# Order of work around the last norms, the memory block's projection and its outputs in a two-layer decoder kernel

## The chip, the cores and the metric

The kernel runs on one core of a Trainium2 chip. The core has TensorE (PE in the profile; PEld is its loading of weights), VectorE (DVE), ScalarE (ACT), GpSimd (POOL) and SyncE (SP, which here issues nearly all transfers). The metric is device time in microseconds, the median over runs.

## The reference, cut to what matters

All is f32, 2048 tokens (32 sequences of 64) of width 512. Four blocks follow each other, each added to x, each fed by a layer norm of x:

```python
x = x + L0_xattn(layernorm(x), ctx)      # 32 query heads, 8 key heads, RoPE, softmax over 64 keys
x = x + L0_ffn(layernorm(x))             # int4 weights, 512 -> 1376 -> 512, silu(gate) * up
x = x + L1_xattn(layernorm(x), ctx)      # q and k with RMS norms per head
x = x + L1_ffn(layernorm(x))             # the memory block:

def L1_ffn(h):
    query = h @ Wq.T                                      # 64 wide
    router = (query @ Wr.T) @ (keys @ Wr.T).T / sqrt(48) + log_rel    # over 128 slots
    top = top_k(router, 8)
    w = softmax(query @ keys.T / 8 + log_rel, over top)
    aux = (w @ values) @ Wvd.T @ Wvu.T
    log_var = log1p(var(h))
    learned = gelu(h @ Wu1.T + bu1) @ Wu2.T + bu2
    u = clip(0.5 * log_var / mean(log_var) + 2.5 * sigmoid(learned), 0, 5)
    gate = sigmoid(w1 * clip((u - 0.5) / 1.5, 0, 1) + bias)   # 0 where under 0.05
    return h + gate * aux
```

The mean of log_var runs over all 2048 tokens, so no gate is known before the last norm.

## The kernel before, in words

The tokens are cut into four chunks of 512 (index c, 0 to 3), each of four tiles of 128 tokens. x stays on the chip. An attention walks 32 steps (g, c): for each of 8 groups g of heads, the four chunks. Large products (the query projection and the output projection) are made as seven half-size products instead of eight (`product`, L179, with PE's matmuls on line L186; `quarters`, L195), which needs sums of blocks of the operands: `left_sums` (L163) and `right_sums` (L171), four additions on POOL each.

One step of `run` (L635) works on several steps at once. In PE's order it has: the rest of the output products of the step before (40 matmuls O), the key projection pk (`project_k`) and the query projection P (56 matmuls, `project_q`) of the next step, the weighted values po of this step (`values`, L554), the small sums pm for the RMS norms of the next step (`norms`, L433), its value projection pv, the first two output products O of this step (16 matmuls, `output_first`), and the scores S of the next step (`scores`, L462). `norms` has DVE add epsilon (qs, L458), POOL raise to the power -1/2 (qr, `rsqrt`, L229) and DVE spread the queries' part to a tile rb (L278). `softmax` (L479) is a generator whose pieces are run between the output products of `output_rest` (L601): it scales S by rb and a key's column (L504), POOL adds the mask (L514), DVE takes the maximum, ACT the exponential (L540), POOL multiplies by the reciprocal sums (L546).

In the last group's steps the chunks are finished one after the other. When chunk c has its last output product, `joined(c)` makes the memory block's values of chunk c-1 (`mem_values`, pwt and paux on PE) and the norm's statistics of chunk c; `after(c)` then runs `norm_apply` (L246) and `mem_weights` (L1009) for chunk c. For chunk 3 both stand behind the attention, and then come the gates and the outputs (`mem_gate`, `mem_out`). `norm_apply` has DVE make a normed tile xn (L251), PE transpose it (L256) and ACT copy it to xnT (L260), and then calls `mem_each` for that tile: DVE's variance of xn (L1002, L1003) and POOL's addition of xn to x (L1004). `mem_weights` projects xnT to qy (pqy, on L1014, copied on L1025) and to the gate's hidden layer (pu, same line), makes the slot scores pr (L1031), the gelu (L1035) and its product with one column (pl, L1038; copied to lrn, L1041), and then the choice of the top eight slots on DVE (L1046 to L1058). `mem_softmax` has DVE take the maximum (L1069) and ACT the exponential (L1072). `mem_mean`, in chunk 3, takes the mean of log_var (L1101 on ACT, L1103 on PE). `mem_out` writes out = aux * gate + x by one DVE instruction a tile (L1148) and sends it (L1151); the 12 tiles of chunks 0 to 2 share gate "a", the four of chunk 3 gate "b", whose aux is still in PSUM.

The program is written with a tile framework. It takes the instructions in program order as priorities, plays them through by a cost model, and so fixes for each engine an order in which that engine issues; an engine then takes its instructions strictly in that order. It also adds the semaphores and gives out buffers. `tc.issue_after(ins)` adds to each instruction of its block that runs on the engine of `ins` the condition that it be ordered behind `ins`; it adds no wait. Tiles of the kind m2 (512 wide) share four buffers.

Of the kernel before, what the change touches and what calls it, by code (L numbers as in the profile page):

```python
# [15 lines left out]
ALU = mybir.AluOpType  # L16
# [28 lines left out]
def tile_xattn_ffn_2_layers(ctx: ExitStack, tc: tile.TileContext, a: dict, out: bass.AP):  # L45
# [125 lines left out]
    def right_sums(t):  # L171
# [4 lines left out]
        tt(b[1], b[3], b[1], ALU.subtract)  # L176
        tt(b[6], b[2], b[5], ALU.subtract)

    def product(which, ps, left, right, widths=(P, P), first=True):  # L179


        l, r = PRODUCTS[which]
        pv = ps.rearrange("p (m n) -> p m n", m=2)
        for m, w in enumerate(widths):
            for k in range(2):
                nc.tensor.matmul(  # L186
                    pv[0:w, m, :],
                    left[:, l, k, m * P : m * P + w],
                    right[:, r, k, :],
                    start=(first and m == 0 and k == 0),  # L190
                    stop=(k == 1),
                    skip_group_check=True,
                )

    def quarters(n, left, right, done, widths=(P, P)):  # L195

# [29 lines left out]

    def rsqrt(dst, src):

        nc.gpsimd.tensor_tensor(dst, src, nhalf[:, : src.shape[-1]], ALU.pow)  # L229

    norms = {}

# [13 lines left out]
    def norm_apply(c, name, each=None):  # L246

        mv, rs = norms[c]
        for t in range(TT):
            xn = m2_tile(f"xn{name}{c}_{t}")  # L250
            ins = nc.vector.tensor_scalar(  # L251
                xn, x_sb[c][:, t, :], mv[:, t, 0:1], rs[:, t : t + 1], ALU.subtract, ALU.mult
            )
            pt = mm_tile(f"xt{name}{c}_{t}")
            for k in range(KT):
                nc.tensor.transpose(  # L256
                    pt[:, k * P : (k + 1) * P], xn[:, k * P : (k + 1) * P], ident
                )
            at = (t % 2) * P
            nc.scalar.copy(  # L260
                xnT[c][:, t // 2 : 4 : 2, :, at : at + P],
                pt.rearrange("p (j k t) -> p j k t", j=2, k=2),
            )
            if each is not None:
                each(c, t, xn)
        if each is None:
            right_sums(xnT[c])
        return ins.ins

# [17 lines left out]
    class Attention:  # L287
        def __init__(self, layer):
            self.L = layer
            self.wq, self.wkv, self.wo = {}, {}, {}  # L290
            self.names = (
                ("L0_wq", "L0_wk", "L0_wv", "L0_wo")
                if layer == 0
                else ("L1_wqT", "L1_wkT", "L1_wvT", "L1_woT")
            )
# [137 lines left out]
        def norms(self, g, c, kpart, part):  # L433


            if self.L == 0:
                return None
            n = f"1_{g}_{c}"
            NQ, NK = NH * GQ * KH, NH * KH

            pm = mm_tile(f"pm{n}")
            k6 = kpart.rearrange("p (x j) -> p j x", j=4)
            p6 = part.rearrange("p i f (j x) -> p j i f x", j=4)
            for j in range(4):
                nc.tensor.matmul(
                    pm[j * KB : (j + 1) * KB, 0:NQ].rearrange("p (f i x) -> p i f x", f=NH, i=2),
                    fold,
                    p6[:, j],
                    start=True,
                    stop=True,  # L450
                )
                nc.tensor.matmul(
                    pm[j * KB : (j + 1) * KB, NQ : NQ + NK], fold, k6[:, j], start=True, stop=True
                )
            qs = sm.tile([P, NQ + NK], F32, tag="qs", name=f"qs{n}")
            qr = sm.tile([P, NQ + NK], F32, tag="qr", name=f"qr{n}")

            nc.vector.tensor_scalar(qs, pm[:, 0 : NQ + NK], HD * EPS, None, ALU.add)  # L458
            rsqrt(qr, qs)
            return spread(f"rb{n}", qr[:, 0:NQ]), qr[:, NQ:]  # L460

        def scores(self, g, c, kT, qT):  # L462
            n = f"{self.L}_{g}_{c}"
# [15 lines left out]
        def softmax(self, g, c, st, scales):  # L479
# [18 lines left out]
                src = s5  # L498
                scale = 1.0 / math.sqrt(HD)
            else:  # L500
                rb, kr = scales
                for f in range(NH):
                    for e in range(KH):
                        nc.vector.scalar_tensor_tensor(  # L504
# [130 lines left out]
        def run(self, hooks, joined, after, between=lambda c: None, tail=lambda: None, late={}):  # L635
# [15 lines left out]
            for i, (g, c) in enumerate(steps):  # L651
# [38 lines left out]
                oT = self.values(g, c, v, probs)  # L690
                if more:
                    scales = self.norms(*steps[i + 1], kpart, part)
                self.pooled = left_sums(oT)
                if more:
                    v = self.project_v(*steps[i + 1], ctxT)
                before = self.output_first(g, c, oT)
                if more:
                    st = self.scores(*steps[i + 1], kT, qT)
                ctxT = ctx_next
            between(NCH - 2)  # L700
            self.output_rest(*before)
# [306 lines left out]

    def mem_weights(c, behind=lambda: None):  # L1009

        def project(ps, w):
            for half in range(2):
                for k in range(KT):
                    nc.tensor.matmul(  # L1014
                        ps[:, half * HC : (half + 1) * HC],
                        w[:, k, :],
                        xnT[c][:, 2 * (k // 2) + half, k % 2, :],
                        start=(k == 0),
                        stop=(k == KT - 1),
                    )  # L1020
# [3 lines left out]
        qy = m2_tile(f"qy{c}")  # L1024
        nc.vector.tensor_copy(qy[0:BOT, :], py[0:BOT, :])  # L1025
        p = mm_tile(f"pu1_{c}")
        project(p, mem["wu1"])
        behind()
        pr = st_tile(f"pr{c}").rearrange("p j (t n) -> p (j t) n", t=2)
        for t in range(TT):  # L1030
            nc.tensor.matmul(  # L1031
                pr[:, t, :], qy[0:BOT, t * P : (t + 1) * P], mem["m2"], start=True, stop=True
            )
        gT = m2_tile(f"gT{c}")
        nc.scalar.activation(gT, p, AF.Gelu_apprx_tanh, bias=mem["bu1"])  # L1035
        pl = mm_tile(f"pl{c}")
        for t in range(TT):
            nc.tensor.matmul(  # L1038
                pl[:, t : t + 1], gT[:, t * P : (t + 1) * P], mem["wu2"], start=True, stop=True
            )  # L1040
        nc.vector.tensor_copy(mem["lrn"][:, c * TT : (c + 1) * TT], pl[:, 0:TT])  # L1041
        bc = [P, TT, NSLOT]
        lr = mem["lr"].unsqueeze(1).to_broadcast(bc)

# [14 lines left out]
            att, left, neg[:, 1:2].unsqueeze(2).to_broadcast(bc)  # L1059
        )  # L1060
        mem["att", c] = att

    def mem_softmax(c, behind=None):
        if behind is not None:
# [68 lines left out]
    def mem_out(name, c0, c1):  # L1133
# [4 lines left out]
        for c in range(c0, c1):  # L1138
            o4 = (
                q_tile(f"o{c}")  # L1140
                if c == 0
                else (o_tile if c == 1 else w_tile)(f"o{c}")[:, 0:4].rearrange("p b h w -> p b (h w)")
            )
            for t in range(TT):
                g = c * TT + t
                col = g - c0 * TT
                o = o4[:, t, :]
                nc.vector.scalar_tensor_tensor(  # L1148
                    o, mem["aux", c, t], gate[:, col : col + 1], x_sb[c][:, t, :], ALU.mult, ALU.add
                )  # L1150
                nc.sync.dma_start(out[g * P : (g + 1) * P, :], o)  # L1151


# [43 lines left out]
    def load_second():  # L1197
# [12 lines left out]
    )  # L1210
    att1.run(
        {(0, 1): [lambda: norm_apply(last, "c")], (1, 0): [lambda: mem_constants(att1.loaded)]},
        lambda c: (mem_values(c - 1) if c > 0 else None, norm_stats(c, "d")),
        lambda c: (norm_apply(c, "d", mem_each), mem_weights(c)),
        lambda c: mem_softmax(c, att1.copied),
    )
    norm_apply(last, "d", mem_each)
    mem_weights(last, mem_mean)
    mem_gate("a", 0, last)
    mem_softmax(last)  # L1220
    mem_values(last)
# [82 lines left out]
```

## Time and profile before

| what | value |
|---|---|
| median of 3 runs | 2943.01 us (2938.76 to 2943.08) |
| the profiled execution | 2943.32 us, of which the span is 2941.5 |
| PE busy | 2838.8 us, 97% |
| mean granted PE clock | 0.987 |
| one ordinary step of the second attention | 36.15 us (pk to pk) |
| last output instruction ends | 2938.31 us |

An instruction's line starts with its start and its duration in us; "xcount" says how many are merged, and the bracket gives the engine's idle time before it and what ended it. Tiles carry their chunk's work in their names: xnd are the normed tiles of the memory block's norm, xtd their transposes. The tail, from about 2750 us on, has chunk 0's norm at 2756, chunk 1's at 2817, chunk 2's at 2865 and chunk 3's at 2905.

### The profile page before, as it was taken

To read this page: it belongs to the slowest core of one execution; us is meant where nothing else is said; L and a number is where in the kernel's file an instruction comes from. 1 tells how busy PE (TensorE), PEld (TensorE's weight loads), DVE (VectorE), ACT (ScalarE), POOL (GpSimd) and SP (SyncE) were. 2 spreads that over 40 slices of the span, in tenths; PEclk is the share of its full clock that TensorE was granted. 3 is DMA by queue.
4 is the path that set the end of the run, shared out by engine and by line. 5 is a ranking of instruction groups with operands and counts; after the bars stand their busy time and mean duration, and the time that the engine had idled before them with its cause. 6 is when DMAs were issued, how large, how long until landed. Compare 5 with 4: busy or idle time off the path is not lost.

```text
span 2941.5 us, 40415 instructions
## 1 busy us (share of the span) xinstructions
PE 2838.8 (97%) x16502; PEld 2217.1 (75%) x16502; DVE 1812.1 (62%) x2752; ACT 820.2 (28%) x1397; POOL 1283.9 (44%) x932
## 2 busy tenths in 40 slices
PE   7999999999999999899999999999999999999987
PEld 5878787778887787676666677777777777787765
DVE  7667777777777766544433665555555555555565
ACT  3323333333333333211111222222222222222232
POOL 5544545454545455411222444444445353535432
PEclk9999999999999999899999999999999999999998
DMA  4111111111111111000000102120202020201001
GB/s 159 40 44 44 52 45 51 49 60 51 45 52 44 51 44 58 23 22 22 20 8 17 36 29 67 34 65 30 65 29 65 30 65 29 65 31 64 15 1 58
DMA packets 103807, 130.71 MB, mean 44 GB/s; under 512 B 8725, under 2 KB 65165, under 8 KB 103623
## 3 DMA queue, kind: packets, MB, share of 16 engines
q1 hardware_dynamic: 103047, 127.09, 13.3%
q8 instruction: 130, 2.13, 0.3%
q10 hardware_dynamic: 576, 1.05, 0.1%
q14 instruction: 54, 0.44, 0.1%
HBM read 123.92 MB, written 4.19 MB: 44 GB/s over the span
## 4 chain that ended last, share of the span: by engine, by line
PE 80%; DVE 12%; ACT 3%; issue 2%; POOL 2%; DMA 0%; DVEq 0%; ACTq 0%; POOLq 0%
PE P L186 30%; PE O L186 22%; PE pv L369 8%; PE pk L339 6%; PE pd L896 5%; PE S L470 4%; DVE part L425 2%; PE po L566 2%; DVE x L592 2%; DVE qT L419 1%; ACT q L421 1%; ACT rq L384 1%; DVE S L493 1%; PE pqy L1014 1%; DVE r2x L525 1%
## 5 line engine op out<-in xcount | busy, mean ns | idle before, releaser
L186 PE MATMUL P<-xnT,wq 128*128 128x256 f32 x3584 | 799.2, 382 | 23.4 <-ACT h L209 21.9
L186 PE MATMUL O<-wo,oT 128*128 128x256 f32 x3584 | 803.8, 382 | 4.2 <-ACT oT L574 3.3
L186 PEld LDWEIGHTS P<-xnT,wq 128*128 128x128 f32 x3584 | 678.8, 191 | 159.2 <-issue 39.2
L186 PEld LDWEIGHTS O<-wo,oT 128*128 128x128 f32 x3584 | 671.4, 190 | 118.0 <-issue 22.1
L592 DVE TENSOR_TENSOR x<-x,O 128x512 f32<-128x512 f32 (+1 forms) x448 | 368.5, 823 | 145.6 <-PE O L186 145.1
L546 POOL TENSOR_TENSOR s<-s,ib 128x512 f32<-128x512 f32 x128 | 169.6, 1347 | 489.0 <-DVE ib L278 480.5
L209 ACT COPY h<-P 128x512 f32<-128x512 f32 (+1 forms) x352 | 200.1, 573 | 365.4 <-PE P L186 354.5
L388 POOL TENSOR_TENSOR qT<-h,rq 128x512 f32<-128x512 f32 x128 | 175.4, 1370 | 277.1 <-DVE rq L387 267.2
L186 PE MATMUL P<-xnT,wgu 128*128 128x256 f32 (+1 forms) x1232 | 273.8, 382 | 0.0
L540 ACT ACTIVATE s<-s 128x1024 f32<-128x1024 f32 x64 | 67.7, 1057 | 708.1 <-DVE s L538 708.1
L186 PEld LDWEIGHTS P<-xnT,wgu 128*128 128x128 f32 (+1 forms) x1232 | 228.0, 187 | 47.1 <-issue 7.4
L229 POOL TENSOR_TENSOR qr<-qs,nhalf 128x20 f32<-128x20 f32 x32 | 113.4, 3543 | 335.0 <-DVE qs L458 335.0
L369 PE MATMUL pv<-wkv,ctxT 128*128 128x128 f32 x1984 | 238.0, 278 | 3.0 <-DVE h L401 1.7
L369 PEld LDWEIGHTS pv<-wkv,ctxT 128*128 128x128 f32 x1984 | 226.2, 192 | 14.0 <-issue 8.6
L384 ACT COPY rq<-h 64x512 f32<-64x512 f32 x256 | 157.9, 617 | 245.3 <-DVE h L401 242.9
L339 PE MATMUL pk<-ctxT,wkv 128*128 128x512 f32 x496 | 223.1, 592 | 0.0
L419 DVE TENSOR_TENSOR qT<-h,P 128x512 f32<-128x512 f32 x128 | 83.9, 674 | 170.4 <-PE P L186 170.4
L885 POOL TENSOR_TENSOR hT<-h,h 128x512 f32<-128x512 f32 (+1 forms) x48 | 55.6, 1179 | 283.4 <-DVE h L878 263.7
L339 PEld LDWEIGHTS pk<-ctxT,wkv 128*128 128x128 f32 x496 | 94.1, 190 | 92.9 <-issue 89.9
L896 PE MATMUL pd<-wd,hT 128*128 128x512 f32 (+1 forms) x352 | 155.0, 592 | 0.0
L386 DVE TENSOR_TENSOR h<-h,cosT 128x512 f32<-128x512 f32 x128 | 90.0, 703 | 105.0 <-ACT rq L384 105.0
L878 DVE TENSOR_TENSOR h<-h,P 128x512 f32<-128x512 f32 (+1 forms) x96 | 59.6, 640 | 151.9 <-PE P L186 103.7
(235 smaller groups left out, 3234.4 us busy)
## 6 DMA issues: line engine op xcount, KB each, us to landing
ctxT<-in_ctxT SPq DMA_DIRECT2D x62, 1024.0 KB
wq<-in_L_wq SPq DMA_DIRECT2D x32, 256.0 KB
wo<-in_L_wo SPq DMA_DIRECT2D x32, 256.0 KB
wq<-in_L_wqT SPq DMA_DIRECT2D x32, 256.0 KB
wo<-in_L_woT SPq DMA_DIRECT2D x32, 256.0 KB
wgu<-in_qweight_gu SPq DMA_DIRECT2D x40, 128.0 KB
out<-o SPq DMA_DIRECT2D x16, 256.0 KB
x<-in_x SPq DMA_DIRECT2D x12, 256.0 KB
```

The costliest lines, as they stand in the source:

```text
L186: nc.tensor.matmul(pv[0:w, m, :], left[:, l, k, m * P : m * P + w], right[:, r, k, :], start=(first and m == 0 and k == 0), stop=(k == 1), ...
L209: nc.scalar.copy(t[size], ps[size])
L229: nc.gpsimd.tensor_tensor(dst, src, nhalf[:, : src.shape[-1]], ALU.pow)
L339: nc.tensor.matmul(ps, wkv[:, k, 0, :], ctxT[:, k, :], start=(k == 0), stop=(k == KT - 1))
L369: nc.tensor.matmul(ps[:, t * HD : (t + 1) * HD], ctxT[:, k, t * P : (t + 1) * P], wkv[:, k, 1, :], start=(k == 0), stop=(k == KT - 1),)
L384: nc.scalar.copy(t[lo:hi, 1], src[HD - hi : HD - lo])
L388: nc.gpsimd.tensor_tensor(dst(None), dst(x), dst(t[:, 1]), ALU.add)
L419: nc.vector.tensor_tensor(q, xv, yv, ALU.add)
L470: nc.tensor.matmul(s5[j * KB : (j + 1) * KB, f, e], kT[:, f, e, j], qT[:, f * 4 + j].rearrange("p h q -> p (h q)"), start=True, stop=True,)
L546: nc.gpsimd.tensor_tensor(sv[:, f], sv[:, f], ib[:, f * W : (f + 1) * W].unsqueeze(1).to_broadcast([P, KH, W]), ALU.mult,)
L592: self.added = nc.vector.tensor_tensor(dst, dst, src, ALU.add).ins
L896: nc.tensor.matmul(p, hT[0:w_, t, tk * P : (tk + 1) * P], wd[i][0:w_, t, :], start=(t == 0), stop=(t == len(tiles) - 1),)
```

## The change

- `norm_apply` with `each` (the memory block's norms alone): all four tiles are normed, transposed and copied first, and `mem_each` is called for the four behind them.
- `mem_weights`: the slot scores pr (and in chunk 3 the mean's part) come between the two halves of the gate's projection pu. The gelu's result lies in block 0 of the chunk's xnT instead of an m2 buffer. Its product pl becomes a function of its own, `mem_learned`, called ahead of the chunk's `mem_values`, that is in `joined(c + 1)`, and for chunk 3 behind `mem_weights`.
- `norms` returns the column tile; the spread rb is made in `softmax`, ordered behind the latest addition of an output product on DVE.
- In `run`, the scores are ordered behind the latest product's last matmul, and in the second attention the sums of oT behind the next step's power on POOL.
- `mem_out`: of gate "a", the first tile of each chunk is made on POOL by two instructions instead of one on DVE.

```diff
     def norm_apply(c, name, each=None):
@@
-            if each is not None:
+            tiles.append(xn)
+        if each is not None:
+            for t, xn in enumerate(tiles):
                 each(c, t, xn)
-        if each is None:
+        else:
             right_sums(xnT[c])
@@ norms
-            rsqrt(qr, qs)
-            return spread(f"rb{n}", qr[:, 0:NQ]), qr[:, NQ:]
+            self.pooled = rsqrt(qr, qs)
+            return qr[:, 0:NQ], qr[:, NQ:]
@@ softmax
-                rb, kr = scales
+                qr, kr = scales
+                if self.added is None:
+                    rb = spread(f"rb{n}", qr)
+                else:
+                    with tc.issue_after(self.added):
+                        rb = spread(f"rb{n}", qr)
@@ run
-                self.pooled = left_sums(oT)
+                if self.L == 1 and more:
+                    with tc.issue_after(self.pooled):
+                        self.pooled = left_sums(oT)
+                else:
+                    self.pooled = left_sums(oT)
@@
-                    st = self.scores(*steps[i + 1], kT, qT)
+                    with tc.issue_after(last_matmul):
+                        st = self.scores(*steps[i + 1], kT, qT)
@@ mem_weights
-        project(p, mem["wu1"])
-        behind()
         pr = st_tile(f"pr{c}").rearrange("p j (t n) -> p (j t) n", t=2)
-        for t in range(TT):
-            nc.tensor.matmul(
-                pr[:, t, :], qy[0:BOT, t * P : (t + 1) * P], mem["m2"], start=True, stop=True
-            )
-        gT = m2_tile(f"gT{c}")
+
+        def scores():
+            behind()
+            for t in range(TT):
+                nc.tensor.matmul(
+                    pr[:, t, :], qy[0:BOT, t * P : (t + 1) * P], mem["m2"], start=True, stop=True
+                )
+
+        project(p, mem["wu1"], scores)
+
+        gT = blocks(c, 0)
         nc.scalar.activation(gT, p, AF.Gelu_apprx_tanh, bias=mem["bu1"])
-        pl = mm_tile(f"pl{c}")
-        for t in range(TT):
-            nc.tensor.matmul(
-                pl[:, t : t + 1], gT[:, t * P : (t + 1) * P], mem["wu2"], start=True, stop=True
-            )
-        nc.vector.tensor_copy(mem["lrn"][:, c * TT : (c + 1) * TT], pl[:, 0:TT])
+        mem["gT", c] = gT
@@
+    def mem_learned(c):
+
+        pl = mm_tile(f"pl{c}")
+        for t in range(TT):
+            nc.tensor.matmul(
+                pl[:, t : t + 1], mem["gT", c][:, t * P : (t + 1) * P], mem["wu2"], start=True, stop=True
+            )
+        nc.vector.tensor_copy(mem["lrn"][:, c * TT : (c + 1) * TT], pl[:, 0:TT])
@@ mem_out
-                nc.vector.scalar_tensor_tensor(
-                    o, mem["aux", c, t], gate[:, col : col + 1], x_sb[c][:, t, :], ALU.mult, ALU.add
-                )
+                if name == "a" and t == 0:
+
+                    aux = mem["aux", c, t]
+                    nc.gpsimd.tensor_scalar(aux, aux, gate[:, col : col + 1], None, ALU.mult)
+                    nc.gpsimd.tensor_tensor(o, aux, x_sb[c][:, t, :], ALU.add)
+                else:
+                    nc.vector.scalar_tensor_tensor(
+                        o, mem["aux", c, t], gate[:, col : col + 1], x_sb[c][:, t, :],
+                        ALU.mult, ALU.add,
+                    )
                 nc.sync.dma_start(out[g * P : (g + 1) * P, :], o)
@@ the calls
-        lambda c: (mem_values(c - 1) if c > 0 else None, norm_stats(c, "d")),
+        lambda c: ((mem_learned(c - 1), mem_values(c - 1)) if c > 0 else None, norm_stats(c, "d")),
@@
     mem_weights(last, mem_mean)
+    mem_learned(last)
     mem_gate("a", 0, last)
```

## The prediction

> **What bounds the kernel now.** I read the page first, then the waits of PE by stretch, then timelines of one ordinary step and of the tail.
>
> ```profile
> PE 2838.8 (97%) x16502; PEld 2217.1 (75%) x16502; DVE 1812.1 (62%) x2752; ACT 820.2 (28%) x1397; POOL 1283.9 (44%) x932
> ...
> PEclk9999999999999999899999999999999999999998
> ```
>
> PE is busy 97% at nearly full clock, so only a PE gap or work after PE's last matmul can be won. The waits of PE, first for second-attention steps without memory work (1700 to 2740 us), columns: total, times, longest:
>
> ```profile
> PE pm L445 <- DVE part L425: 10.9, 29, 0.6
> ```
>
> and for the tail (2740 to 2942):
>
> ```profile
> PE xtd L256 <- DVE xnd L251: 10.9, 5, 4.6
> PE xtd L256 <- DVE vst L1003: 6.0, 4, 2.0
> PE pwt L1083 <- ACT xnT L1072: 5.7, 1, 5.7
> PE paux L1088 <- ACT wT L1085: 4.0, 4, 1.3
> PE O L186 <- ACT oT L574: 2.1, 1, 2.1
> PE pl L1038 <- ACT gT L1035: 0.7, 3, 0.3
> ```
>
> 29 ordinary steps share 10.9 us of waits that the change doesn't touch; the last 200 us hold 29.4. An ordinary step in the timeline:
>
> ```profile
> 2254.57 0.71 DVE L278 STREAM_TRANSPOSE rb<-qr 128x512 f32<-128x512 f32 x1 [3.66 <-POOL qr L229]
> ...
> 2256.18 0.69 DVE L592 TENSOR_TENSOR x<-x,O 128x512 f32<-128x512 f32 x1 [0.90 <-PE O L186]
> ...
> 2257.80 1.93 PE L470 MATMUL S<-qT,kT 128*32 128x256 f32 x32
> ...
> 2257.91 0.69 DVE L592 TENSOR_TENSOR x<-x,O 128x512 f32<-128x512 f32 x1 [1.04 <-PE O L186]
> ...
> 2259.80 1.66 DVE L504 SCALAR_TENSOR_TENSOR s<-S,qr,rb 128x256 f32<-128x256 f32 x4 [1.21 <-PE S L470]
> ```
>
> S already stands behind the second product, POOL's power (2251.00) ahead of the sums of oT (2254.51).
>
> **The pins and the moved spread: 0.** The spread rb goes behind the second addition (ends 2258.60), so it ends at 2259.31; S ends at 2259.73, L504 starts at 2259.80. Its cover is 0.4 us. Without it L504 comes up to 0.7 us later, still off PE: the weights are ready at 2275.0, and po needs them at about 2284 (15.7 us behind pk, as one step earlier). The sums wait for the power as they do now, layer 0's scores stand behind the second product already, and no DMA moves.
>
> **Norm tiles first.** Chunk 2 in the timeline:
>
> ```profile
> 2864.97 1.00 DVE L251 TENSOR_SCALAR xnd<-x,mvd,rsd 128x512 f32<-128x512 f32 x2 [1.14 <-POOL rsd L229]
> ...
> 2865.59 2.73 POOL L1004 TENSOR_TENSOR x<-x,xnd 128x512 f32<-128x512 f32 x2 [0.66 <-DVE xnd L251]
> ...
> 2867.16 1.45 DVE L251 TENSOR_SCALAR xnd<-x,mvd,rsd 128x512 f32<-128x512 f32 x1
> ```
>
> The third tile takes 1.45 us instead of 0.5: it is through only when POOL's additions are, at 2868.32. DVE and POOL exclude each other here. Around 1707 us three such tiles ran against four POOL operations, taking turns: 3.67 us for three, POOL 1.45 each instead of 1.27. The variances (L1002, 0.65 each) no longer stand between, but POOL's additions still start with the first tile. So the fourth tile is gained only in part. Chunks 0 and 1: its end goes from 2761.24 to about 2760.1, -1.15 each. Chunk 2: third tile -1.2, fourth -0.3, PE transposing at half clock between: -0.7. Chunk 3: -0.45. Sum **-3.45** (ends 0, if the turns fall otherwise, and -6, if POOL never got in the way). The variances end about 1 us later (chunk 3: 2912 instead of 2910.9); behind them Ln has its result near 2914, and PE asks for it after half the gate's projection, near 2915.3.
>
> **Slot scores amid the projection, gelu's product later.** Each half of the projection takes 1.86 us. pr (1.99) needs qy, copied 0.8 us after the first projection: ready. The top-eight chain on DVE starts 1.86 earlier and gelu 1.99 later, which nothing waits for any more. PE no longer waits for gT: **-0.7** (last row of the waits). pl (1.05, 8 matmuls) moves, it doesn't vanish: for chunk 0 it goes between two busy stretches (0); for chunk 1 into the 4.6 us in which PE waits for chunk 2's norm (-1.05); for chunk 2 either into the gap before O or ahead of pwt, where it is paid again (-1.05 or 0; I take -0.5). Sum **-1.55**. In chunk 2 an exponential of the gate (L1116, waiting for lrn until 2885.64) stands ahead of ACT's oT copies: they start at 2885.76, though po ended at 2884.79 and an ordinary step has 0.07 between. With lrn made later that goes: **-0.9** (0 if pl stays early). The earlier top-eight chain brings power, mask and exponential about 1 us earlier against PE, so wT is no longer behind it on ACT: two paux waits fall from 1.28 to the 0.73 seen at 2902.17, and chunk 2's statistics gain some 0.5: **-1.6** (ends 0, -2.2).
>
> **The end.** In chunk 3 pr ends at 2919.56, its DVE chain sets the exponential, PE's 5.7 us wait and the outputs. It will come ahead of half a projection (1.86); I take 0.25 off, because PE then changes operands twice: **-1.6** beside the norm's share (ends 0, if DVE is held otherwise, and -1.86).
>
> From 2926.42 DVE writes the outputs without a break:
>
> ```profile
> 2935.59 2.73 DVE L1148 SCALAR_TENSOR_TENSOR o<-paux,g_gateb,x 128x512 f32<-128x512 f32 x4 [0.24 <-DVE g_gateb L1137]
> ```
>
> 16 of them take 11.9 us to 2938.31, then 3.2 us for the last transfer. Three go to POOL: -2.1. But each becomes two POOL operations: an addition of 1.27 (L1004) and a scaling that has no row. Its nearest rows are the two-input 128x512 at 1.27 above and a one-input 128x128 selection at 0.30 below (four of them 1.2); I take 1.2, ends 0.3 and 1.27. Six make 7.4 us. A DVE form like the output's, two tensors and a scalar column, shows what they do to it, once free and once against POOL's L546:
>
> ```profile
> 348.04 0.70 DVE L745 SCALAR_TENSOR_TENSOR scales_gu<-scales_gu,pidx 12x512 f32<-12x512 bf16 x1
> ...
> 350.18 1.64 DVE L745 SCALAR_TENSOR_TENSOR scales_gu<-scales_gu,pidx 12x512 f32<-12x512 bf16 x1
> ```
>
> So the POOL operations hold up outputs and gate b's small scalings between them. Of 7.4 about 1.0 overlaps (a held one ends 0.54 behind POOL, not 0.70): +6.4. With the three outputs saved: **+4.3** (ends -2.1 and +5.3). SP issues the 16 transfers in order, 0.33 each; POOL is through about 10 us after the gate, 6 before the last output, so its three hold up none at the end. The Trainium skill (GPSIMD Engine Reference, Elementwise — side-by-side cycle accounting) gives 769 ns for its best loop on 512 elements; by that estimate the three scalings are 1.3 us cheaper and the sum 1.3 lower. No run here shows it.
>
> **The clock.** Columns: PE, PEld, DVE, ACT, POOL busy, granted clock, DMA, GB/s.
>
> ```profile
> 2754.40:2767.30 12.90, 8.53 (x34) 5.42 (x33) 7.65 (x16) 3.60 (x6) 5.33 (x4) 0.74 0.00 1
> ...
> 2884.80:2891.30 6.50, 4.44 (x12) 3.52 (x13) 3.98 (x14) 3.79 (x13) 3.36 (x3) 0.74 0.00 0
> ```
>
> After gaps of 2.17 and 0.92 the clock lost 0.26 x 12.9 = 3.4 us, after one of 2.07 1.7 us. Chunk 0, chunk 1 and the O gap lose 8.5 together. Shorter gaps should save part: **-1.5** (ends -6 and +1.7, one stretch more). The Trainium skill (TensorE: Matmul & The Clock Gate, What's actually happening) has the slow clock come after an idle window of about 3.4 us. By that rule gaps of 2 us would cost nothing and this term would be 0, the sum 2937.8; the second row, slow after a gap of 2.07 us, speaks against it, and 2937.8 lies in the forecast's own range.
>
> **Sum.** -3.45 - 1.55 - 0.7 - 0.9 - 1.6 - 1.6 - 1.5 + 4.3 = -7.0. The profiled execution took 2943.3 (span 2941.5 and 1.8 around it), 0.3 above the median of 2943.0: 2943.3 - 7.0 = **2936.3**.
>
> **Rivals.** *POOL costs nothing at the end*: its operations fall beside outputs without holding them, end term -2.1: 2943.3 - 11.3 - 2.1 = 2929.9. For it: 12 output rows ran with no POOL beside them, so this line never met it; against: L745. *Gains given back*: only norm tiles, gelu wait and pl count (-5.7), because the order on DVE and ACT in the tail puts other waiting work in front, and the end takes its full +5.3: 2942.9. For it: ACT's L1116 shows such queueing now. *Slower*: the pin says only that S comes behind the second product. If S drifts behind all of O, it moves 8.7 us (2259.7 to 2268.4), and the 9.0 us that the softmax weights now have before po shrink to 0.3. On its way stand 7 us of DVE work for q and k; if that adds 1.2, PE waits 0.9 in each of 31 steps: 2936.3 + 28 = 2964. It decides for slower from 0.42 us a step, (2949.2 - 2936.3) / 31. Against: S now stands there unpinned in every ordinary step.
>
> **Chances.** About 0.2% (5.9 us) is what a measurement of this kernel tells from no change: the three times spread over 4.3. Forecast 0.50 (own range 2931 to 2941), end free 0.14, given back 0.27, S late 0.09. Faster than 2937.1: 0.36 of the forecast, 0.13 of the second, 0.03 of the third: 0.52. Slower than 2948.9: 0.09 and 0.02 of given back: 0.11. Within: 0.37. Range 2930 to 2945: it takes in the first three.
>
> **What would show it.** S still behind 16 O matmuls and rb behind the second L592; four xnd in about 3.8 us with POOL's additions stretched; pr between two runs of eight pu; no PE wait for gT; oT copies right behind po in chunk 2; 13 DVE outputs, several of 1.3 to 2 us, beside six POOL operations. I am wrong if the outputs keep 0.74 us, if PE's wait for xnd or the clock's slow stretches grow, or if ordinary steps are no longer 36.15 us.

## The result, and the profile after

The changed kernel takes **2932.76 us** (median of 7 runs, 2929.51 to 2934.91); the kernel before 2941.91 (7 runs, 2938.76 to 2943.36). The ratio is 0.9969, with a 95% interval of 0.9958 to 0.9981: 9.1 us less, between 5.6 and 12.4. The prediction was 2936.3, 7.0 less. The profiled execution took 2932.82, with a span of 2931.0; before it was 2943.32 and 2941.5.

The page of the changed kernel, engines and clock:

```profile
PE 2837.0 (97%) x16502; PEld 2215.4 (76%) x16502; DVE 1811.8 (62%) x2749; ACT 819.9 (28%) x1397; POOL 1292.6 (44%) x938
...
PEclk9999999999999999899999999999999999999998
```

PE does the same matmuls in 1.8 us less. POOL has six instructions more and 8.7 us more. The waits of PE, first in the ordinary steps (1700 to 2735 us), columns: total, times, longest:

```profile
PE pm L453 <- DVE part L433: 10.7, 29, 0.4
```

That was 10.9 before: nothing has happened there. Then in the tail (2735 to 2931):

```profile
PE xtd L261 <- DVE xnd L256: 11.3, 10, 2.9
PE paux L1116 <- ACT wT L1113: 2.8, 4, 0.7
PE pl L1086 <- ACT xnT L1059: 2.1, 1, 2.1
PE pwt L1111 <- ACT xnT L1100: 1.6, 1, 1.6
PE O L189 <- ACT oT L587: 1.1, 1, 1.1
PE xtd L261 <- ACT xnT L265: 0.8, 1, 0.8
```

These are 19.7 us where 29.4 stood. The wait for the variances (vst, 6.0) is gone; the transposes wait for scaled tiles and, once, 0.8 us for a copy to xnT. The wait for the exponential in chunk 3 (pwt) went from 5.7 to 1.6, with a new one of 2.1 ahead of it: pl, now behind the gelu, waits for it. In chunks 0 to 2 that wait is gone.

Chunk 2's norm in the timeline of the changed kernel (start, time, engine, line, work; in brackets what was waited for):

```profile
2856.65 3.83 DVE L256 TENSOR_SCALAR xnd<-x,mvd,rsd 128x512 f32<-128x512 f32 x4 [1.13 <-POOL rsd L233]
2857.27 5.56 POOL L1022 TENSOR_TENSOR x<-x,xnd 128x512 f32<-128x512 f32 x4 [0.66 <-DVE xnd L256]
...
2857.34 1.08 PE L261 MATMUL xtd<-ident,xnd 128*128 128x128 f32 x8 [2.89 <-DVE xnd L256]
...
2859.21 1.09 PE L261 MATMUL xtd<-ident,xnd 128*128 128x128 f32 x4 [0.79 <-ACT xnT L265]
...
2860.39 1.27 DVE L1020 BATCH_NORM_STATS2 st<-xnd 128x6 f32<-128x512 f32 x2
```

The four tiles follow each other, but need 3.83 us, as POOL's additions begin 0.6 us behind the first. From the first scaled tile to the first matmul of pqy the four chunks took 6.46, 6.47, 5.66 and 4.86 us before, and take 5.16, 5.16, 4.99 and 4.54 now.

At the end, the outputs on DVE, with the small operations of gate b between them:

```profile
2912.54 0.75 DVE L1182 SCALAR_TENSOR_TENSOR o<-xnT,g_gatea,x 128x512 f32<-128x512 f32 x1
...
2915.61 0.74 DVE L1182 SCALAR_TENSOR_TENSOR o<-xnT,g_gatea,x 128x512 f32<-128x512 f32 x1
...
2917.00 1.23 DVE L1145 TENSOR_SCALAR g_sgb<-g_sgb 128x4 f32<-128x4 f32 x1
2918.14 1.83 DVE L1182 SCALAR_TENSOR_TENSOR o<-xnT,g_gatea,x 128x512 f32<-128x512 f32 x1
...
2923.99 2.73 DVE L1182 SCALAR_TENSOR_TENSOR o<-paux,g_gateb,x 128x512 f32<-128x512 f32 x4 [0.24 <-DVE g_gateb L1165]
```

and POOL beside them:

```profile
2912.60 3.95 POOL L1179 TENSOR_SCALAR xnT<-xnT,g_gatea 128x512 f32<-128x512 f32 x2 [13.13 <-DVE g_ub L1152]
2916.52 2.90 POOL L1180 TENSOR_TENSOR o<-xnT,x 128x512 f32<-128x512 f32 x2
2919.41 2.00 POOL L1179 TENSOR_SCALAR xnT<-xnT,g_gatea 128x512 f32<-128x512 f32 x1
2921.49 1.44 POOL L1180 TENSOR_TENSOR o<-xnT,x 128x512 f32<-128x512 f32 x1
```

The first output starts at 2912.5, where it started at 2926.4: **13.9 us earlier**, of which 2.0 were there already as the tail began. But 13 outputs now last 14.2 us where 16 lasted 11.9, and the span ends 4.3 us behind the last of them, not 3.2. So the end gives back 3.4 us, and the span is 10.5 shorter. The transfers between 2910 and 2931 us, busy share and GB/s in slices of 0.525 us:

```profile
DMA  0000000092000000069999999999999999999000
GB/s 0 0 0 0 0 0 0 12 378 109 0 0 0 0 0 0 0 257 382 382 378 382 375 378 406 371 379 382 382 375 382 375 386 394 382 375 363 4 0 0
```

One tile leaves, then nothing for 4 us: the second in SP's order is POOL's first, which is ready only at 2918.2. From there 15 tiles go without a gap at some 380 GB/s.

### The profile page after: what moved, and what is told of

Its sections match the earlier page's. It is cut to its first block, busy times and chain, and to the rows that moved or that the text cites. A ratio compares the mean times of both kernels' runs of the same rounds, so it can differ in the third digit from the quotient of the medians.

```text
span 2931.0 us, 40439 instructions
## 1 busy us (share of the span) xinstructions
PE 2837.0 (97%) x16502; PEld 2215.4 (76%) x16502; DVE 1811.8 (62%) x2749; ACT 819.9 (28%) x1397; POOL 1292.6 (44%) x938
## 3 DMA queue, kind: packets, MB, share of 16 engines
HBM read 123.92 MB, written 4.19 MB: 44 GB/s over the span
## 4 chain that ended last, share of the span: by engine, by line
PE 80%; DVE 12%; ACT 3%; issue 2%; POOL 2%; DMA 0%; DVEq 0%; ACTq 0%; POOLq 0%
PE P L189 30%; PE O L189 23%; PE pv L377 8%; PE pk L347 6%; PE pd L914 5%; PE S L478 4%; DVE part L433 2%; PE po L579 2%; DVE x L605 2%; DVE qT L427 1%; ACT q L429 1%; ACT rq L392 1%; DVE S L501 1%; PE pqy L1034 1%; DVE r2x L538 1%
```

## The experiments

**The theory**: the two changes ahead of the gates bring what the traces show, and POOL's outputs cost about 4 us, because POOL and DVE hold each other up. **The rivals**: POOL is free and the lost time belongs to gates that come closer together; the end is made by SP's queue behind POOL's tile; the pins or the moved share of the spread bring the 2 us ahead of the tail.

**All outputs on VectorE in the changed kernel** (one instruction for each tile, as before; the expectation's brackets make it two, and its 16 tiles are those of all four chunks together).

```diff
-                if name == "a" and t == 0:
-                    aux = mem["aux", c, t]
-                    nc.gpsimd.tensor_scalar(aux, aux, gate[:, col : col + 1], None, ALU.mult)
-                    nc.gpsimd.tensor_tensor(o, aux, x_sb[c][:, t, :], ALU.add)
-                else:
-                    nc.vector.scalar_tensor_tensor(
...
+                nc.vector.scalar_tensor_tensor(
...
```

> The changed kernel, with all 16 of a chunk's output tiles scaled and added on VectorE as before (a scaling and an addition on VectorE for each). In the changed kernel's trace the last four gate products ended 14.2 us earlier than before, while the outputs after them kept only part of that: VectorE needed 14.2 us for its 13 tiles where it needed 11.9 for 16, and the transfers ended 4.3 us after the last output instead of 3.2. Theory (GpSimd's six instructions hold VectorE back, and its first tile holds the output queue): without them the end is 3 to 4 us earlier than in the changed kernel, so about 12 to 13 us below the kernel before, 2929 to 2930 us. Rival (GpSimd is free beside VectorE, and the loss at the end is the gate products coming closer together): VectorE has three tiles more to do, and the time is 1 to 2 us above the changed kernel's, about 7 to 8 us below the kernel before.

Measured: 2929.1 us, 0.9957 of the kernel before (0.9945 to 0.9970), so 12.6 us less. Its outputs:

```profile
2917.94 3.40 DVE L1176 SCALAR_TENSOR_TENSOR o<-xnT,g_gatea,x 128x512 f32<-128x512 f32 x5
2921.86 2.73 DVE L1176 SCALAR_TENSOR_TENSOR o<-paux,g_gateb,x 128x512 f32<-128x512 f32 x4 [0.24 <-DVE g_gateb L1165]
```

They begin at 2912.69, 0.16 later than in the changed kernel, take 11.9 us again, and the span ends at 2927.8, 3.2 earlier. The loss at the end was POOL's: the time is the 2929 to 2930 that was expected, not the rival's 1 to 2 us above the changed kernel.

**Only POOL's outputs, in the kernel before.** The same lines the other way round; POOL gets three of the 16 tiles in all, one each of chunks 0 to 2.

> The kernel before, in which only the last outputs are changed: three of the 16 tiles of each chunk go to GpSimd (a scaling and an addition each), VectorE does 13 in one instruction each for the addition as before. Theory of the prediction: the six instructions cost VectorE 6.4 us and save it three tiles, 2.1 us, so 4.3 us longer than the kernel before; as the changed kernel's trace has it, 3 to 4 us longer. Rival (GpSimd free): 2 us shorter than the kernel before.

Measured: 2945.34 us, 1.0015 (1.0006 to 1.0024): 4.4 us **slower**, between 1.8 and 7.1. POOL has the same times as in the changed kernel:

```profile
2922.76 3.95 POOL L1151 TENSOR_SCALAR xnT<-xnT,g_gatea 128x512 f32<-128x512 f32 x2 [14.49 <-DVE g_gatea L1137]
2926.67 2.90 POOL L1152 TENSOR_TENSOR o<-xnT,x 128x512 f32<-128x512 f32 x2
```

From the first output to the end of the span it is 18.5 us, against 15.1 in the kernel before. The free POOL is refuted from both sides.

**POOL's three transfers from POOL's own queue**, in the changed kernel.

```diff
-                nc.sync.dma_start(out[g * P : (g + 1) * P, :], o)
+                q = nc.gpsimd if name == "a" and t == 0 else nc.sync
+                q.dma_start(out[g * P : (g + 1) * P, :], o)
```

> The changed kernel, in which the transfers of GpSimd's three output tiles are issued from GpSimd's own queue and the other 13 from the common one, so that no tile of VectorE waits behind one of GpSimd. In the changed kernel the second transfer was issued at 2918.2 us, 4.9 us after the first, and from there 15 transfers followed one another at 380 GB/s to the end. Theory A (the blocked queue makes the end): the transfers spread over the 5 us, the end is that of the slowest producer, and the time is 1 to 3 us below the changed kernel's. Theory B (VectorE being held by GpSimd makes the end): its last output still comes at the same time, 14.2 us after its first, and only the 1.1 us between the two kernels' last transfers can be had: within 1.1 us of the changed kernel.

Measured: 2930.53 us, 0.9967 (0.9954 to 0.9979), the changed kernel's 0.9969 within the error. The transfers do spread (2905 to 2932 us, slices of 0.675):

```profile
DMA  0000000000001859568400599999759999500000
GB/s 0 0 0 0 0 0 0 0 0 0 0 0 64 325 212 358 206 261 340 176 0 0 206 355 337 385 358 385 304 206 358 379 382 388 228 0 0 0 0 0
```

but DVE's outputs still last 14.3 us, and the span ends 3.75 us behind them instead of 4.28. Theory B holds: the blocked queue is real, but worth about half a microsecond in these two traces, which is less than the times can tell.

**Only the pins and the moved spread, in the kernel before** (the conditions on left_sums, the next scores and rb).

```diff
-            return spread(f"rb{n}", qr[:, 0:NQ]), qr[:, NQ:]
+            return qr[:, 0:NQ], qr[:, NQ:]
...
+                    with tc.issue_after(self.added):
+                        rb = spread(f"rb{n}", qr)
...
+                    with tc.issue_after(last_matmul):
+                        st = self.scores(*steps[i + 1], kT, qT)
```

> The kernel before, in which only the pinned order of the steps and the moved shares of the spread work are taken over. Theory of the prediction: they were put at 0, and the changed kernel's tail began 2 us earlier, which is as much as the stretches of slow clock in the first part of the two traces differ; so within 1 us of the kernel before. Rival: the 2 us before the tail come from the moved shares, and this kernel is about 2 us faster.

Measured: 2942.19 us, 1.0004 (0.9995 to 1.0012). Nothing that can be told from zero, and the pk that opens the tail (the last but one) starts at 2738.75, where it started at 2738.65 before and at 2736.64 in the changed kernel. The 2.0 us ahead of the tail are therefore a difference between two executions; the trace with the norm's order alone (next) is 3.8 us ahead at about 1720 us, where that order isn't in use yet.

**Only the norm's order, in the kernel before.**

```diff
+            tiles.append(xn)
-            if each is not None:
-                each(c, t, xn)
+        if each is not None:
+            for t, xn in enumerate(tiles):
+                each(c, t, xn)
```

> The kernel before, in which only the last norm's order is changed: the four scaled tiles first, then the variances and sums, in all four chunks. Theory of the prediction: 1.15 us each in chunks 0 and 1, 0.7 in chunk 2 and 0.45 in chunk 3, 3.45 us faster in all. What the changed kernel's trace shows beside it: its first matmuls of the gate came 1.3 us earlier in each of the first two chunks, 0.67 in chunk 3 and 0.73 in chunk 4 over the transposes before, which sums to some 4 us. Rival: the two variances and the sums, now behind the tiles, delay the projection's eviction by as much as the transposes gain, and the time is the one before.

Measured: 2934.08 us, 0.9979 (0.9970 to 0.9988): 6.2 us less, between 3.5 and 8.8. In its trace the four stretches from scaled tile to pqy are 5.17, 5.16, 4.99 and 4.53 us: 3.6 us less in all (chunk 2 gains 0.67 and chunk 3 0.33; the expectation counts these two from one). In this pair of traces 1.5 more lie elsewhere in the tail, 0.8 of them between chunk 1's paux and chunk 2's first transpose (8.3 to 7.5), and 3.9 ahead of the tail, where the two kernels do the same. PE's clock from that pk to the first output is 0.92 in both. The wait that this part can't touch stands as before:

```profile
PE pwt L1086 <- ACT xnT L1075: 5.7, 1, 5.7
PE paux L1091 <- ACT wT L1088: 3.5, 4, 1.3
```

**Only the scores and the moved product, in the kernel before.**

```diff
-        project(p, mem["wu1"])
-        behind()
...
+        project(p, mem["wu1"], scores)
...
-        gT = m2_tile(f"gT{c}")
+        gT = blocks(c, 0)
...
-        lambda c: (mem_values(c - 1) if c > 0 else None, norm_stats(c, "d")),
+        lambda c: ((mem_learned(c - 1), mem_values(c - 1)) if c > 0 else None, norm_stats(c, "d")),
```

> The kernel before, in which only the last attention's memory step is changed: the slot scores between the two halves of the gate's projection, the gelu's values kept in the chunk's block and their product one step later, next to the attention values of that step. The prediction gave these parts 0.7 for the wait for the gelu, 1.55 for the moved product, 0.9 for the values no longer ahead of the O projection in chunk 2, 1.6 for the waits of the values and chunk 2's statistics, and 1.6 for chunk 3's earlier scores: 6.35 in all. The comparisons so far leave 9.15 - 6.2 + 4.4 = 7.3 us for it. Theory: 6 to 8 us faster than the kernel before, and in its trace no wait for the gelu in chunks 0 to 2. Rival: the norm's part and this one shorten the same waits, so that the norm's 6.2 us hold part of this one's gain, and alone it brings 3 us or less.

Measured: 2932.15 us, 0.9975 (0.9966 to 0.9985): 7.4 us less. The waits:

```profile
PE xtd L256 <- DVE xnd L251: 8.7, 5, 2.9
PE xtd L256 <- DVE vst L1003: 6.9, 4, 2.0
PE paux L1098 <- ACT wT L1095: 2.8, 4, 0.7
PE pl L1068 <- ACT xnT L1041: 2.1, 1, 2.1
PE pwt L1093 <- ACT xnT L1082: 1.6, 1, 1.6
```

The waits for the variances stay, pwt and paux are those of the changed kernel. The rival's shared gain doesn't show: alone the parts bring -6.2, -7.4, +4.4 and +1.2, together -8.0, against -9.1 for the whole. Each of these is known to within 3 us, so a small share can't be ruled out.

**Only the moved product, in the kernel before.** From the kernel above:

```diff
-        project(p, mem["wu1"], scores)
+        project(p, mem["wu1"])
+        scores()
```

> The kernel before, in which only the gelu's product is moved one step later (with its values kept in the chunk's block); the slot scores stay behind both halves of the gate's projection. With the scores moved too it was 7.35 us faster by the ratio. By the prediction's terms this part brings 0.7 for the wait for the gelu, 1.55 for the product, 0.9 for the copies in chunk 2 and most of the 1.6 for the waits of the values and chunk 2's statistics, 4 to 5 us, and the scores the remaining 2 to 3. Rival: the scores come 1.2 us earlier against their projection in the first chunk's trace and 1.7 in the last's, so they bring more than half, and this part alone 3 us or less.

Measured: 2936.55 us, 0.9986 (0.9977 to 0.9995): 4.1 us less, the theory's 4 to 5. That leaves 3.2 for the scores, but both times are known only to some 2.7 us; the traces tell more. Its waits:

```profile
PE pwt L1094 <- ACT xnT L1083: 5.1, 1, 5.1
PE paux L1099 <- ACT wT L1096: 2.8, 4, 0.7
PE O L186 <- ACT oT L574: 1.1, 1, 1.1
```

The product alone mends paux and O; pwt needs the scores. The starts on PE say where. From chunk 3's pqy to its pwt it is 16.2 us before, 15.6 with the product, 14.3 with both. From chunk 1's paux to chunk 2's first transpose it is 8.3, 7.9 and 6.6. Each of these stretches gains 1.3 by the scores.

**What POOL's additions to x cost.** With all outputs on VectorE, line L1022 is left out, so that the output lacks this term:

```diff
-        nc.gpsimd.tensor_tensor(x_sb[c][:, t, :], x_sb[c][:, t, :], xn, ALU.add)
```

> The changed kernel with all outputs on VectorE, which also leaves out GpSimd's addition of the last norm's tiles to x (the sum that the gated memory is added to), in all four chunks, so its output lacks that term. In the changed kernel the four scaled tiles of a chunk take VectorE from 2753.9 to 2757.9 and from 2856.6 to 2860.5, 3.9 us, with single tiles of 1.1 to 1.5 us where GpSimd adds beside them and 0.5 where it doesn't. Theory (the additions hold VectorE's tiles back, and the transposes wait for these): four tiles take 2 us, the first matmul of the gate comes 1.4 to 1.9 us earlier in each of the four chunks, and the time is 5 to 7 us below that of the kernel with all outputs on VectorE, 2922 to 2924 us. Rival (the transposes and their copies, 0.6 us each on ScalarE, or the variances that follow bound the step): 0 to 2 us.

Measured: 2921.04 us, 0.9936 (0.9924 to 0.9948), 8 us under the kernel with the additions by the medians and 6.2 by the ratios. Four tiles take 2.47, 2.47, 1.92 and 1.91 us, and the first matmul of pqy comes 2.0, 0.9, 0.8 and 1.7 us earlier, 5.4 in all. PE's granted clock from the last but one pk to the first output is 0.97, where it was 0.94 with the additions. The additions cost as much as the norm's new order brought.

**The additions in reverse order**, in the program text only, with all outputs on VectorE and in place of L1022:

```diff
+            for t in reversed(range(TT)):
+                nc.gpsimd.tensor_tensor(x_sb[c][:, t, :], x_sb[c][:, t, :], tiles[t], ALU.add)
```

> The changed kernel with all outputs on VectorE, in which GpSimd adds the last norm's four tiles to x in the reverse order, so that its first addition waits for the fourth tile, and the other three are behind it on GpSimd. Nothing is left out. Theory (as for the kernel without these additions): VectorE's four tiles are undisturbed and the first matmul of the gate comes 1.4 to 1.9 us earlier in each chunk; the additions now lie beside the variances and the eviction of the gate's first projection, which comes later by up to 2 us, and costs at most half of the gain: 3 to 6 us below the kernel with all outputs on VectorE, 2923 to 2926 us. Rival: what VectorE wins on the tiles it loses on the four variances and that eviction, which the scores wait for: within 1 us of it.

Measured: 2929.68 us, 0.9965 (0.9951 to 0.9978). The rival's number, but not for its reason. POOL in chunk 1:

```profile
2811.55 1.27 POOL L274 TENSOR_TENSOR x<-x,xnd 128x512 f32<-128x512 f32 x1 [15.61 <-DVE xnd L256]
2813.18 4.15 POOL L274 TENSOR_TENSOR x<-x,xnd 128x512 f32<-128x512 f32 x3 [0.36 <-DVE xnd L256]
```

and DVE:

```profile
2810.96 0.51 DVE L256 TENSOR_SCALAR xnd<-x,mvd,rsd 128x512 f32<-128x512 f32 x1
...
2812.01 2.96 DVE L256 TENSOR_SCALAR xnd<-x,mvd,rsd 128x512 f32<-128x512 f32 x3
```

POOL still begins as soon as tile 0 is there: the framework put the tile that is ready first at the head of POOL's order. The run says nothing on the question, and the order has to be written out.

**The additions pinned behind the fourth tile**, otherwise as in the last run:

```diff
+            fourth = None
+            for t in reversed(range(TT)):
+                if fourth is None:
+                    fourth = nc.gpsimd.tensor_tensor(
+                        x_sb[c][:, t, :], x_sb[c][:, t, :], tiles[t], ALU.add
+                    )
+                else:
+                    with tc.issue_after(fourth.ins):
+                        nc.gpsimd.tensor_tensor(
+                            x_sb[c][:, t, :], x_sb[c][:, t, :], tiles[t], ALU.add
+                        )
```

> The changed kernel with all outputs on VectorE, in which GpSimd's addition of the fourth tile of the last norm is issued first and the other three are pinned behind it, so that none of the four runs before the fourth tile is scaled (in the run with the order only reversed in the program text, GpSimd still took tile 0 first, 0.1 us after it was scaled, so that run changed next to nothing). Leaving the additions out altogether brought 8 us by the medians, 6 by the ratios. Theory (the cost is the additions lying beside the scaled tiles): the first matmul of the gate comes 1.4 to 1.9 us earlier in each chunk and the additions lie beside the variances, which come later by some 2 us and hold the eviction of the gate's first projection only if they end behind its matmuls, 3.7 us after the first: 3 to 6 us below the kernel with all outputs on VectorE. Rival (the additions hold VectorE back by the same 3 us wherever they lie, and the scores wait for VectorE all the same): within 1.5 us of it.

Measured: **2921.21 us, 0.9935** (0.9922 to 0.9947), with nothing left out: 7.9 us below the kernel with all outputs on VectorE by the medians and 6.5 by the ratios, more than the theory's 3 to 6. Chunk 2:

```profile
2852.96 1.91 DVE L256 TENSOR_SCALAR xnd<-x,mvd,rsd 128x512 f32<-128x512 f32 x4 [1.13 <-POOL rsd L233]
...
2854.79 1.27 DVE L1031 BATCH_NORM_STATS2 st<-xnd 128x6 f32<-128x512 f32 x2
2854.95 1.27 POOL L276 TENSOR_TENSOR x<-x,xnd 128x512 f32<-128x512 f32 x1 [2.03 <-DVE xnd L256]
...
2856.19 2.49 POOL L281 TENSOR_TENSOR x<-x,xnd 128x512 f32<-128x512 f32 x2
2856.20 1.27 DVE L1031 BATCH_NORM_STATS2 st<-xnd 128x6 f32<-128x512 f32 x2
```

Four tiles in 1.91 us, not 3.83. And the variances run beside POOL's additions at their own pace, 1.27 for two, with POOL at its 1.27 as well. The theory had the variances come late by the additions and the rival had VectorE held wherever they lie; neither happens. From the first tile to pqy it is now 3.17, 4.26, 4.19 and 2.94 us. As without the additions, the clock up to the first output is 0.97: part of the gain is PE's higher clock.

**The sum made on ScalarE**, as x (1 + r) - m r:

```diff
+            nc.gpsimd.tensor_scalar(up, rs, 1.0, None, ALU.add)
+            nc.gpsimd.tensor_tensor(off, mv[:, :, 0], rs, ALU.mult)
+            nc.gpsimd.tensor_scalar(off, off, -1.0, None, ALU.mult)
+            with tc.issue_after(copied.ins):
+                for t in range(TT):
+                    nc.scalar.activation(
+                        x_sb[c][:, t, :], x_sb[c][:, t, :], AF.Identity,
+                        bias=off[:, t : t + 1], scale=up[:, t : t + 1],
+                    )
```

> The changed kernel with all outputs on VectorE, in which the sum of x and the last norm's tile is made by ScalarE from x alone, as x (1 + r) - m r with r and m of each token (one activation of a tile, pinned behind the norm's copies; GpSimd makes the two factors, three instructions of 128x4). Nothing is left out. Theory (GpSimd's additions hold VectorE): VectorE's tiles take 0.5 us each as in the kernel without the additions, ScalarE's four activations of some 0.6 us lie in its idle time before the gelu, and the time is within 2 us of the kernel without the additions, 2919 to 2923 us, some 0.6 to 0.7% below the kernel before. Rival (ScalarE's queue is late: the logarithm of the last chunk's variances and the other copies come behind the activations, 2.4 us a chunk): half of that gain is lost in the last chunk and the time is 2924 to 2927 us.

Measured: 2921.19 us, 0.9935 (0.9922 to 0.9947), the same as pinned. ACT in chunk 3:

```profile
2887.78 2.95 ACT L280 ACTIVATE x<-x,off,up 128x512 f32<-128x512 f32 x4
2890.75 1.28 ACT L1139 ACT_TABLE_LOAD   x1
2892.04 0.22 ACT L1139 ACTIVATE g_lv<-vst 128x16 f32<-128x16 f32 x1
```

The logarithm does come behind the four activations, as the rival said, but costs nothing that the time shows. Its tiles take as long as the pinned kernel's, but pqy follows the first after 3.17, 3.17, 2.62 and 2.86 us: in this execution the clock stayed full from 2738.67 to 2899.57 us, while the pinned one's transposes of chunk 2 ran at half clock (16 in 3.57 us instead of 2.00). The profiled execution is the fastest of its five and the medians are equal, so this is no difference between the two kernels. Both versions beat the kernel before by 0.65% and the changed one by about 0.34%.

## Why the prediction was right, and where it was off

**The norm's tiles: right, and by its mechanism.** Terms of 1.15, 1.15, 0.7 and 0.45, 3.45 in all; the trace has 1.30, 1.31, 0.67 and 0.32, 3.6. That POOL stays in the way was foreseen. The outer bound of 6 "if POOL never got in the way" was too small: the pinned run's stretches are 8.9 us below those of before, though part of that is transposes at a higher clock.

**The pins and the spread: 0 foreseen, 1.2 measured with zero in its interval.** In the changed kernel's ordinary step rb lies behind the second addition and ends at 2257.20, before S does; L517 still waits for S (0.59 us of idle time on DVE, until 2257.79), as in the working.

**Gelu, product, copies, statistics, scores: foreseen 6.35, measured 7.4**, the second with this part's share of the clock in it. The gelu's wait of 0.7 is gone in chunks 0 to 2, oT's copies start right behind po in chunk 2 (2875.10, po ends at 2875.08) and the two paux waits are 0.7. Chunk 3's earlier scores were put at 1.6 (the 0.25 taken off for PE's change of operands has no row of its own); from pqy to pwt it is 1.8 to 1.9, 0.6 of it by the product. What was undersized is what earlier scores do for chunk 2's statistics, 1.3 of the 1.7 between chunk 1's paux and chunk 2's transposes; the working allowed some 0.5 there.

**The clock: 1.5 foreseen.** From the start of the tail to the first output, columns: length, then PE, PEld, DVE, ACT and POOL busy, clock, DMA. Before:

```profile
2737.30:2926.40 189.10, 160.24 (x854) 119.58 (x852) 112.16 (x265) 59.00 (x110) 60.37 (x45) 0.92 0.00 1
```

After:

```profile
2735.30:2912.50 177.20, 158.20 (x855) 117.09 (x854) 115.83 (x265) 59.22 (x112) 60.63 (x45) 0.95 0.00 1
```

As many matmuls take 2.0 us less at a clock of 0.95 instead of 0.92. Single executions scatter by more than that. From the last but one pk to the first output, PE is busy for 158.9, 159.0 and 156.4 us in three executions with the old work there (before, the pins, POOL's outputs alone), and for 156.9, 155.3 and 156.9 with the new (changed, own queue, outputs on VectorE). The means are about 1.8 apart, so the size of the term holds, but that this one pair agrees is partly luck. In it the window is 11.9 us shorter; without these 2.0 that is 9.9, and the other terms ahead of the end came to 9.8. The changed kernel's chunk 2 also shows the clock falling: the first eight transposes, behind a wait of 2.89 us, take 0.13 each, the next four, behind another of 0.79, take 0.27. The granted clock is 1.00 from 2855.62 to 2859.03 and 0.50 in the 3.42 us after; PE had worked for 1.08 of the 3.41 us ahead of the fall. In the kernel before it fell so at 2887.87, behind 3.41 us with 1.34 of PE work. The Trainium skill (TensorE: Matmul & The Clock Gate, What's actually happening) has the slow state come after an idle window of about 3.4 us; these two traces have it after as long a stretch in which PE worked for a third of the time or more.

**The end: the amount held, two steps of its working did not.** Foreseen +4.3; measured +4.4 in the kernel before, +3.4 in the trace of the changed kernel. One failed step is "of 7.4 about 1.0 overlaps". POOL's six operations took 10.3 us (a scaling 1.8 to 2.1 where 1.2 was taken, an addition 1.25 to 1.7), and less than half of that held DVE. The 13 outputs sum to 12.5 us where 13 of the kind of before (0.742) make 9.6, so 2.8, and four small operations of gate b took 2.6 instead of 0.8, so 1.8; less three outputs saved, 2.2, that is 2.4 us on DVE. The other step is "its three hold up none at the end": POOL's first tile, second in SP's order, held the queue until 2918.2, when four finished tiles of DVE stood behind it; and POOL was through 3.8 us before the last output, not 6. The transfers then ended 1.1 us later behind the last output than before. The queue's share of that is about half, by the run with POOL's own queue. The errors cancelled: that the term's size came out is luck. The Trainium skill's 769 ns for the scaling (GPSIMD Engine Reference, Elementwise — side-by-side cycle accounting) would have made the sum 1.3 lower; the scalings here took 1.84 to 2.12 us, all with DVE beside them.

**The sum**: -7.0 foreseen, -9.1 measured, with the first inside the interval of the second. By the two traces, from the tail's start on: 0.1 more ahead of the end, 0.5 more by the clock, 0.9 less lost at the end, so -8.5. The other 0.6 of the medians is below what they resolve. Of the rivals, POOL free at the end named 2929.9, about what the kernel with no outputs on POOL at all takes; that is a coincidence, as its reason, a POOL that costs nothing, is refuted. Gains given back and S late did not occur.

## What to carry to other kernels

An idle engine isn't a free one: before work goes to POOL, look which DVE instructions it will lie beside. Beside scalings and two-tensor forms it cost about 4 us here and six to eight more through additions that were old and looked hidden, beside variances nothing. So put POOL's work next to DVE instructions that don't meet it, pin that order, and look in the trace that the pin has taken. And before a tail is shared between engines, take its transfers as a bound: the 16 tiles, 4.2 MB at 380 GB/s, need 11.0 us, and DVE alone 11.9, so that by this estimate a perfect helper had 0.9 us to win.

## What the runs showed of the hardware

A DVE scaling of 128x512 took 0.5 us alone and up to 1.5 beside a POOL addition; a variance (BATCH_NORM_STATS2) of the same tile took 0.65 to 0.69 beside one as without it, and the additions kept their 1.27. The prediction had said only that the two engines exclude each other. The Trainium skill (SBUF — State Buffer, SBUF: two separate sides) says that DVE and GpSimd lock a pair of ports against each other for a whole instruction, on DVE's side in its two-port modes or with two inputs from SBUF. The traces agree for the scalings and the outputs, and for the variances, which have one input and went on undisturbed. That the scalings use a two-port mode, and the variances none, is not shown by any run.

The four outputs that read paux from PSUM took 2.73 us in all, as before, but POOL was through by then, so what they would do beside it stays open. A small operation is held as long as a large one: a 128x4 form took 1.23 us instead of 0.17.
